# Attention scores from two float32r halves of q and k, projected with doubled weight columns

## The chip, the cores and the metric

The kernel runs on one core of one Trainium2 chip. The metric is the device time of one execution in microseconds (us). The engines are TensorE (PE, matrix products), VectorE (DVE), ScalarE (ACT, one function per element, with a bias and a scale), GpSimd (POOL) and SyncE (SP, which issues most transfers). Matrix products go to PSUM, eight banks of 512 float32 per partition; everything else lies in SBUF.

## The reference

Two layers follow each other: an attention over a weighted adjacency, and a graph network of three SAGE layers on a thinned adjacency. The change concerns the scores of the attention:

```python
x: (16, 1024, 128)   adj: (16, 1024, 1024)   H, HD = 8, 16
q = (x @ Wq.T + bq).reshape(bt, n, H, HD).transpose(0, 2, 1, 3)
k = (x @ Wk.T + bk).reshape(bt, n, H, HD).transpose(0, 2, 1, 3)
v = (x @ Wv.T + bv).reshape(bt, n, H, HD).transpose(0, 2, 1, 3)
scores = jnp.einsum('bhnd,bhmd->bhnm', q, k) / math.sqrt(HD)
scores = jnp.where((adj == 0)[:, None, :, :], -jnp.inf, scores)
attn = jax.nn.softmax(scores, axis=-1) * adj[:, None, :, :]
attn = attn / (attn.sum(axis=-1, keepdims=True) + 1e-08)
ctx = jnp.einsum('bhnm,bhmd->bhnd', attn, v)      # then ctx @ Wo.T + bo
...
adj_d = _dilate(adj, mask)     # neighbours removed row by row, in order
h1 = _bn(relu(_sage(h0, adj_d, ...)))             # and h2, h3 likewise
return concat(h1, h2, h3) @ Wl + bl
```

Here x of the attention is the layer-normalised and rectified input. The removal of neighbours (dilation) needs the adjacency alone, so the kernel computes it beside the attention.

## The kernel before

`swept` does all of it in one pass. The attention goes over 256 turns: batch b (16), half c of the queries (2), block m of 128 keys (8). Each turn has two half-turns, one for each group g of four heads (heads 2j + g, j = 0 to 3). A half-turn does, in this order:

- `scores`: 16 small bfloat16 matmuls (L554) lay -1e30 on the pairs without an edge, from `never` and `nomask`; then four float32 matmuls (L560), one for each row group of 32 rows, add k times q. The 32 rows of a row group hold two heads. `qT` holds q twice, for g = 0 and g = 1, each with the rows of the other head set to zero by the scale `own`. The result fills two tiles of two banks each, all that the pool `ps_s` has.
- other work that was queued: for g = 0 the four transposes of the adjacency block of two turns later (`turn_over`, L505) into the one bank of `ps_m`; for g = 1 one step of the list `beside`.
- `values`: for the half-turn before, the value columns of each head times w (L487) and the sums of e (L492).
- two exponentials on ACT (L598, e from the scores), two products on DVE (L603, w = e times the turned adjacency). e and w have four buffers each, so two half-turns.
- for g = 0, on ACT, the copy of the turned block out of its bank (L508) and the mask `nomask` from it (L512).

Work for the next batch stands in generators on the list `beside`. Each yields the kind of place at which it wants to go on, and `go_on_with` continues the first whose kind fits: `True` is the place behind the scores of the second half-turn, "evict" the place behind the products, `False` the end of a half-turn. `prepare` makes layer norm, the transpose hT, and for each half c the projections `key` (L322, evicted by L324 on ACT into kT), `value` (L333) and `query` (L312, evicted twice by L315 on ACT into qT). `conclude` turns and projects the finished half (L395 copies the two accumulators, L401, L414, L424, and L429 adds to the input on DVE). All of these go through the one bank of `ps_m`, except in the first batch.

The dilation is another generator. `beside_attention` continues it behind each half-turn as long as its planned cost lies behind the share of the half-turns that are done. Its largest rows on ACT are L915 and L909, on DVE L900, L922 and L925.

After the attention, `judge` counts what would make the one pass invalid (an adjacency value that is not as assumed, a removal that had not settled, a softmax sum out of range) and sets a flag. If the flag is set, the whole slower program `walked` runs behind. Then come the three SAGE layers.

Of the kernel before, what the change touches and what calls it, by code (L numbers as in the profile page):

```python
# [10 lines left out]
F32 = mybir.dt.float32  # L11
BF = mybir.dt.bfloat16
F16 = mybir.dt.float16
# [8 lines left out]
P = 128  # L22
# [12 lines left out]
def swept(ctx: ExitStack, tc: tile.TileContext, t: dict, out: bass.AP, flag: bass.AP):  # L35
# [131 lines left out]
    def first_part(p1):  # L167
# [32 lines left out]
        names = ("Wk", "Wv", "Wq", "Wo")  # L200
        raw = pool.tile([P, 4, D], F32, name="raw", tag="kT")
        for i, name in enumerate(names):
            nc.sync.dma_start(raw[:, i, :], t[f"L0_gnn_{name}"])
        attn_w = one.tile([P, 4, D], F32, name="attn_w")
        wts = {name: attn_w[:, i, :] for i, name in enumerate(names)}
        bk = one.tile([P, 1], F32, name="bk")
        nc.sync.dma_start(bk, t["L0_gnn_bk"].rearrange("(d o) -> d o", o=1))

        own = one.tile([P, 2], F32, name="own")
        nc.vector.tensor_reduce(  # L210
            own,
            ident.rearrange("p (j g d) -> p g j d", g=2, d=HD),
            AX.XY,
            ALU.add,
        )
        bq = one.tile([P, 3], F32, name="bq")
        nc.sync.dma_start(bq[:, 2:3], t["L0_gnn_bq"].rearrange("(d o) -> d o", o=1))
# [3 lines left out]
        def turn_weights():  # L221
            wps = ps_d.tile([P, 4, D], F32, name="wps", tag="d")
            for i in range(4):
                nc.tensor.transpose(wps[:, i, :], raw[:, i, :], ident)
            yield
            nc.vector.tensor_copy(attn_w, wps)
            nc.vector.tensor_tensor(bq[:, 0:2], own, bq[:, 2:3].to_broadcast([P, 2]), ALU.mult)
            yield
# [15 lines left out]
        both = shared.tile([P, 4096], F32, name="both", tag="aT2")  # L244
# [8 lines left out]
        ]  # L253
        never = one.tile([P, P], BF, name="never")
# [37 lines left out]
        def prepare(b):  # L292
# [15 lines left out]
            kT = pool.tile([P, N], F32, name=f"kT_{b}", tag="kT")  # L308

            def query(c, bank=(ps_m, "m")):  # L310
                pq = bank[0].tile([P, 512], F32, name=f"pq_{b}_{c}", tag=bank[1])
                nc.tensor.matmul(pq, wts["Wq"], hT[:, c * HN : (c + 1) * HN], start=True, stop=True)  # L312
                yield "evict"
                for g in range(2):
                    nc.scalar.activation(  # L315
                        qTs[c][:, g, :], pq, AF.Identity, bias=bq[:, g : g + 1], scale=own[:, g : g + 1]
                    )

            def key(c, bank=(ps_m, "m")):
                cc = slice(c * HN, (c + 1) * HN)  # L320
                pk = bank[0].tile([P, 512], F32, name=f"pk_{b}_{c}", tag=bank[1])
                nc.tensor.matmul(pk, wts["Wk"], hT[:, cc], start=True, stop=True)  # L322
                yield "evict"
                nc.scalar.activation(kT[:, cc], pk, AF.Identity, bias=bk)  # L324
# [17 lines left out]
            if b == 0:  # L342
# [13 lines left out]
                yield from key(0)  # L356
                qTs = [pool.tile([P, 2, HN], F32, name=f"qT_{b}_0", tag="qT")]
                yield from query(0, (ps_d, "d"))
                yield from second
                ready[b] = (xt, qTs, kT, v1)  # L360
# [3 lines left out]
                yield from turned(1)  # L364
            else:
# [4 lines left out]
                for what in (key, value):  # L370
                    yield True
                    yield from what(0)

                yield "half 1"
                qTs = [pool.tile([P, 2, HN], F32, name=f"qT_{b}_0", tag="qT")]
                yield True
                yield from query(0)

            ready[b] = (xt, qTs, kT, v1)
            for what in (key, value):  # L380
                yield True
                yield from what(1)
            yield "half 0"
            qTs.append(pool.tile([P, 2, HN], F32, name=f"qT_{b}_1", tag="qT"))
            yield True
            yield from query(1)

        def conclude(b, c, acc, xt):

            yield False  # L390
            cx = small.tile([P, HB, H, HD], F32, name=f"cx_{b}_{c}", tag="cx", bufs=1)
# [78 lines left out]
        def go_on_with(*kinds):  # L470


            for steps in beside[::-1] if kinds == ("first",) else beside:
                if steps[1] in kinds:
                    steps[1] = next(steps[0], None)
                    if steps[1] is None:
                        beside.remove(steps)
                    return

        def attention():  # L480
# [58 lines left out]
            def scores(i, g):  # L539
# [4 lines left out]
                _, qTs, kT, _ = ready[b]  # L544
                nomask = tiles[i][1]
                mm = slice(m * P, (m + 1) * P)
# [11 lines left out]
                for j in range(4):  # L558
                    rows = slice(32 * j, 32 * j + 32)
                    nc.tensor.matmul(  # L560
                        scs[j // 2][:, j % 2, :], kT[rows, mm], qTs[c][rows, g, :],
                        start=False, stop=True, tile_position=(32 * j, 0),
                    )
# [3 lines left out]
            for i, (b, c, m) in enumerate(turns):  # L567
# [12 lines left out]
                for g in range(2):  # L580
# [6 lines left out]
                    else:  # L587
                        go_on_with(True)
                    if late:
                        values(*late)  # L590
                    elif g == 0:
# [21 lines left out]
                    go_on_with(False)  # L613
                    if i + g + 1 < len(turns):
# [36 lines left out]
        def dilation():  # L651
# [84 lines left out]
            for k in range(NB):  # L736
# [150 lines left out]
                wrs, gms, ers, ets = {}, {}, {}, {}  # L887
# [8 lines left out]
                for i in range(B + 2):  # L896
# [15 lines left out]
                    if b < B:  # L912
                        wrs[b] = pool.tile([P, N], F16, name=f"wr_{k}_{b}", tag="wr", bufs=2)
# [1061 lines left out]
```

## Time and profile before

| What | us |
|---|---|
| median of 3 runs (lowest, highest) | 3412.89 (3412.76, 3414.29) |
| the profiled execution | 3414.15 |
| its span | 3412.3 |
| PE busy | 3316.5 (97%) |
| DVE busy | 2967.2 (87%) |
| ACT busy | 2328.2 (68%) |
| mean granted TensorE clock | 0.995 |

The profile is of one execution. Busy times are unions over the span; matmuls are pipelined and their ends are modelled, so the time that a group of matmuls takes is better read from start to start. The page shows 40 slices of 85.3 us with the busy tenths of each engine. A row of a group names line, engine, operation, output and inputs, shapes and count, then the busy time in us and the mean ns of one, then the idle time just before and what ended it. The attention takes the span up to about 2345 us; the SAGE layers take the rest.

### The profile page before, as it was taken

The numbers are of one execution on the slowest core, as the hardware profiler recorded it, in microseconds if no ns is written. First come the engines' busy times: TensorE is split into PE (matmuls) and PEld (weight loads), VectorE is DVE, ScalarE is ACT, GpSimd is POOL, SyncE is SP. The second block draws the span as 40 slices with busy tenths as digits, with TensorE's granted clock in tenths as the row PEclk, the third lists the DMA queues.
The fourth block names the chain that finished last, engine by engine and source line by source line (L and its number), as shares of the span: only waits on it lengthen the run. The fifth ranks groups of instructions, "written<-read, shape, count | busy, mean of one in ns | idle before, by whom it ended". The sixth has DMA issues, their size and how long they took to land. (4 is left out here: it accounts for less than half of the span.)

```text
span 3412.3 us, 86211 instructions
## 1 busy us (share of the span) xinstructions
PE 3316.5 (97%) x34855; PEld 1870.2 (55%) x34855; DVE 2967.2 (87%) x5271; ACT 2328.2 (68%) x3909; POOL 163.8 (5%) x253
## 2 busy tenths in 40 slices
PE   8999999999999999999999999999999899999997
PEld 3333333333333333333334334336999899999997
DVE  7888988988889898998988999897888799988887
ACT  7699689779879969968976986884222344433324
POOL 2000000000000000000000000000000000000000
PEclk9999999999999999999999999999999999999999
DMA  7366456547637745845863783677999799989996
GB/s 240 109 173 203 129 149 199 159 128 218 188 122 211 219 123 174 242 144 150 244 188 120 230 246 119 190 239 258 338 335 338 276 350 352 349 325 351 353 351 219
DMA packets 650122, 772.27 MB, mean 226 GB/s; under 512 B 173264, under 2 KB 569168, under 8 KB 637424
## 3 DMA queue, kind: packets, MB, share of 16 engines
q1 hardware_dynamic: 632672, 708.58, 64.2%
q0 software_dynamic: 15456, 57.30, 5.0%
q8 instruction: 275, 4.51, 0.6%
q14 instruction: 135, 1.11, 0.1%
q10 hardware_dynamic: 1584, 0.79, 0.1%
HBM read 508.50 MB, written 157.29 MB: 195 GB/s over the span
## 5 line engine op out<-in xcount | busy, mean ns | idle before, releaser
L603 DVE TENSOR_TENSOR w<-e,aT 128x1024 f32<-128x1024 f32 x1024 | 1206.1, 1219 | 193.3 <-ACT e L598 191.8
L598 ACT ACTIVATE e<-sc 128x1024 f32<-128x1024 f32 x1024 | 992.0, 1023 | 327.3 <-PE sc L560 326.2
L1129 PE MATMUL pg<-y,aT 128*128 128x128 f32 (+1 forms) x6144 | 729.8, 275 | 0.0
L1129 PEld LDWEIGHTS pg<-y,aT 128*128 128x128 f32 x6144 | 707.9, 192 | 0.0
L560 PE MATMUL sc<-qT,kT 32*128 32x512 f32 x4096 | 583.9, 640 | 0.5 <-ACT qT L315 0.5
L487 PE MATMUL acc<-w,both 128*32 128x512 f32 x4096 | 574.4, 605 | 5.8 <-DVE w L603 5.2
L492 PE MATMUL acc<-e,eps 128*32 128x512 f32 x4096 | 561.3, 593 | 0.0
L146 DVE SCALAR_TENSOR_TENSOR aT<-mr,aT 128x1024 f32<-128x1024 bf16 x384 | 458.9, 1217 | 0.0
L492 PEld LDWEIGHTS acc<-e,eps 128*32 128x32 f32 x4096 | 144.1, 110 | 299.7 <-issue 294.8
L1152 ACT ACTIVATE sq<-o 128x512 f32<-128x512 f32 x96 | 60.6, 631 | 356.1 <-DVE o L1147 356.1
L554 PE MATMUL sc<-nomask,never 32*32 32x512 bf16 x8192 | 268.0, 384 | 35.1 <-ACT e L598 32.0
L554 PEld LDWEIGHTS <-never 32*32 32x32 bf16 x8192 | 87.3, 87 | 376.5 <-issue 354.1
L1170 ACT COPY hT<-pt 128x512 f32<-128x512 f32 x96 | 56.4, 587 | 267.6 <-PE pt L1166 259.1
L560 PEld LDWEIGHTS sc<-qT,kT 32*128 32x128 f32 x4096 | 159.9, 182 | 116.9 <-issue 116.1
L505 PEld LDWEIGHTS pa<-ident,a 128*128 128x128 f32 x1024 | 107.7, 141 | 181.2 <-issue 126.7
L915 ACT ACTIVATE wr<-both,th 128x512 f16<-128x512 f16 x256 | 205.1, 879 | 1.7 <-DVE both L900 1.5
L505 PE MATMUL pa<-ident,a 128*128 128x128 f32 x1024 | 168.3, 287 | 6.5 <-DMA a<-in_adj 5.8
L487 PEld LDWEIGHTS acc<-w,both 128*32 128x32 f32 x4096 | 88.4, 108 | 150.4 <-issue 50.4
L512 ACT ACTIVATE nomask<-aT 128x512 bf16<-128x512 f32 x256 | 161.3, 630 | 8.3
L1147 DVE SCALAR_TENSOR_TENSOR o<-pg,rdeg,mine 128x128 f32<-128x128 f32 x384 | 108.2, 345 | 56.5 <-PE pg L1129 53.2
L508 ACT COPY aT<-pa 128x512 f32<-128x512 f32 x256 | 153.0, 598 | 5.0 <-PE pa L505 4.3
L900 DVE TENSOR_TENSOR_SCAN both<-rk 128x513 f16<-128x513 bf16 x128 | 155.9, 1218 | 0.0
(228 smaller groups left out, 3830.2 us busy)
## 6 DMA issues: line engine op xcount, KB each, us to landing
aT<-aT_d SPq DMA_DIRECT2D x94, 2048.0 KB, 9.9
mr<-mr_d SPq DMA_DIRECT2D x188, 512.0 KB, 6.2
aT_d<-aT SPq DMA_DIRECT2D x256, 256.0 KB, 4.3
a<-in_adj SPq DMA_DIRECT2D x253, 256.0 KB, 4.3
ad<-in_adj SPq DMA_DIRECT2D x112, 512.0 KB, 4.4
nomask<-nomask SPq DMA_DIRECT2D x512, 96.0 KB, 2.7
nomask<-nomask SPq DMA_DIRECT2D x512, 64.0 KB, 2.9
nomask<-nomask SPq DMA_DIRECT2D x512, 32.0 KB, 2.9
```

The costliest lines, as they stand in the source:

```text
L146: nc.vector.scalar_tensor_tensor(part, mrs[h][:, j : j + 2, :].rearrange("p j n -> p (j n)"), 0.0, part, ALU.is_equal, ALU.mult)
L487: nc.tensor.matmul(acc[g][32 * j : 32 * j + 32, :], v1[:, m, (2 * j + g) * HW : (2 * j + g) * HW + 32], ws[j // 2][:, j % 2, :], start=(m ...
L492: nc.tensor.matmul(acc[g][32 * j : 32 * j + 32, :], eps8, es[j // 2][:, j % 2, :], start=False, stop=(m == NB - 1),)
L505: nc.tensor.transpose(pa[:, k * P : (k + 1) * P], a[:, k, :], ident)
L512: nc.scalar.activation(nomask[:, 0, :], aT[:, 0, :], AF.Relu, bias=1.0, scale=-1e38, accum_out=zeros[:, i : i + 1])
L554: nc.tensor.matmul(scs[j // 2][to : to + 32, j % 2, :], never[rows, rows], nomask[rows, j, :], start=True, stop=False, tile_position=(32 * ...
L560: nc.tensor.matmul(scs[j // 2][:, j % 2, :], kT[rows, mm], qTs[c][rows, g, :], start=False, stop=True, tile_position=(32 * j, 0),)
L598: nc.scalar.activation(e, scs[q], AF.Exp, scale=1.0 / math.sqrt(HD))
L603: nc.vector.tensor_tensor(w, es[q], aT.to_broadcast([P, 2, HN]), ALU.mult)
L900: nc.vector.tensor_tensor_scan(pair_sums[b % 2], row[:, 0::2], row[:, 1::2], 0.0, ALU.add, ALU.add)
L915: nc.scalar.activation(wrs[b][:, t::2], pair_sums[b % 2][:, t : t + HN], AF.Abs, bias=at[:, b : b + 1], scale=2.0,)
L1129: nc.tensor.matmul(pg[:, i // 2, at : at + width], aT[:, j, i * P : (i + 1) * P], y[:, j, :width], start=(j == 0), stop=(j == NB - 1),)
```

## The change

q and k are kept as float32r, which the kernel takes for a float32 that is rounded when an engine writes it. Each number is held as a rounded high half and a residual, itself rounded. For this the projection weights of q and k are laid out anew by `twofold`: for each group g a matrix whose 32 columns of a row group hold one head's 16 columns twice. One projection per group then puts a head on both halves of the 32 rows. For k the upper 16 rows hold the rounded value and the lower 16 the residual (`key_halves`; `low_rows` is 1 on the lower rows). For q the high half stands on all 32 rows in one tile and the residual on all 32 in another (`query_halves`). The scores then are two matmuls per row group, k with q's high half and k with q's residual, eight in all instead of four, each with float32r operands.

So every projection of q and k is done twice, once for each group, and each is evicted by ACT (the rounded value) and then by DVE (value minus rounded value). In the schedule a projection's first matmul is issued at a new place, "end", at the end of a first half-turn; its eviction is at "early", in front of the exponentials of the second half-turn; its second matmul at "behind", after that half-turn's values; and the second eviction at "evict". `value` of the second half now goes ahead of `key` of the second half. To make room, the concluded context (`cx_home`) and the new weights lie in the tile `both`, and two tiles of the dilation share one (`pair`). `judge` also rounds a sample on ACT and on DVE and sets the flag where the two differ.

```diff
+        both = shared.tile([P, 4096], F32, name="both", tag="aT2")
+        one_w = one.tile([P, 2, D], F32, name="one_w")
+        two_w = both[:, 4096 - 4 * D :].rearrange("p (i d) -> p i d", d=D)
+        wts = {name: one_w[:, i, :] for i, name in enumerate(("Wv", "Wo"))}
+        wts |= {name: two_w[:, i, :] for i, name in enumerate(("q0", "q1", "k0", "k1"))}
+        bqk = one.tile([P, 4, 2], F32, name="bqk")
+        def twofold(dst, w):
+
+            for g in range(2):
+                of_g = w.rearrange("p (j g d) -> p g j d", g=2, d=HD)[:, g]
+                nc.vector.tensor_copy(
+                    dst[:, g, :].rearrange("p (j i d) -> p j i d", i=2, d=HD),
+                    of_g.unsqueeze(2).to_broadcast([P, 4, 2, HD]),
+                )
...
+            bps = ps_o.tile([P, HN], F32, name="bps", tag="acc0")
+            for g in range(2):
+                nc.tensor.matmul(
+                    bps[:, 2 * g : 2 * g + 2], twice_ident[:, g, :], bqk[:, 0, :], start=True, stop=True
+                )
-            nc.vector.tensor_copy(attn_w, wps)
-            nc.vector.tensor_tensor(bq[:, 0:2], own, bq[:, 2:3].to_broadcast([P, 2]), ALU.mult)
+            twofold(two_w[:, 2:4, :], wps[:, 3, :])
+            twofold(two_w[:, 0:2, :], wps[:, 2, :])
+            nc.vector.tensor_copy(one_w, wps[:, 0:2, :])
+            nc.vector.tensor_copy(bqk[:, 1:3, :].rearrange("p g t -> p (g t)"), bps[:, 0:4])
+            nc.vector.tensor_scalar(bqk[:, 3, :], bqk[:, 1:3, 1], low_rows, None, ALU.mult)
...
+        free += 2 * (HN // 2 + 1)
+        cx_home = both[:, free : free + HN]
+        twice_ident = shared.tile([P, 2, P], F32, name="twice_ident", tag="s", bufs=2)
+        twofold(twice_ident, ident)
...
-            kT = pool.tile([P, N], F32, name=f"kT_{b}", tag="kT")
-
-            def query(c, bank=(ps_m, "m")):
-                pq = bank[0].tile([P, 512], F32, name=f"pq_{b}_{c}", tag=bank[1])
-                nc.tensor.matmul(pq, wts["Wq"], hT[:, c * HN : (c + 1) * HN], start=True, stop=True)
-                yield "evict"
+            qs, ks = [], []
+
+
+
+            def query_halves(c, g, ps):
+                if g == 0:
+                    qs.append(pool.tile([P, 2, 2, HN], F32R, name=f"q_{b}_{c}", tag="qM"))
+                high, low = (qs[c][:, g, i, :] for i in range(2))
+                bias = bqk[:, 1 + g, 0:1]
+                nc.scalar.activation(high, ps, AF.Identity, bias=bias)
+                nc.vector.scalar_tensor_tensor(low, ps, bias, high.bitcast(F32), ALU.add, ALU.subtract)
+
+            def key_halves(c, g, ps):
+                if g == 0:
+                    ks.append(pool.tile([P, 2, HN], F32R, name=f"k_{b}_{c}", tag="kA", bufs=3))
+                half = ks[c][:, g, :]
+                nc.scalar.activation(half, ps, AF.Identity, bias=bqk[:, 3, g : g + 1], scale=low_rows)
+                nc.vector.scalar_tensor_tensor(
+                    half, ps, bqk[:, 1 + g, 1:2], half.bitcast(F32), ALU.add, ALU.subtract
+                )
+
+            def both_groups(name, halves, c, banks):
                 for g in range(2):
-                    nc.scalar.activation(
-                        qTs[c][:, g, :], pq, AF.Identity, bias=bq[:, g : g + 1], scale=own[:, g : g + 1]
+                    where, tag = banks[g % len(banks)]
+                    ps = where.tile([P, 512], F32, name=f"p{name}_{b}_{c}_{g}", tag=tag)
+                    nc.tensor.matmul(
+                        ps, wts[f"{name}{g}"], hT[:, c * HN : (c + 1) * HN], start=True, stop=True
                     )
-
-            def key(c, bank=(ps_m, "m")):
-                cc = slice(c * HN, (c + 1) * HN)
-                pk = bank[0].tile([P, 512], F32, name=f"pk_{b}_{c}", tag=bank[1])
-                nc.tensor.matmul(pk, wts["Wk"], hT[:, cc], start=True, stop=True)
-                yield "evict"
-                nc.scalar.activation(kT[:, cc], pk, AF.Identity, bias=bk)
+                    yield ("early", "evict")[g]
+                    halves(c, g, ps)
+                    if g == 0:
+                        yield "behind"
+
+            def query(c, banks=((ps_m, "m"),)):
+                yield from both_groups("q", query_halves, c, banks)
+
+            def key(c, banks=((ps_m, "m"),)):
+                yield from both_groups("k", key_halves, c, banks)
...
             else:
                 yield from layer_norm_relu(h, xt, f"a{b}")
                 for c in range(2):
                     yield True
                     yield from turned(c)
-                for what in (key, value):
-                    yield True
-                    yield from what(0)
-
+                yield "end"
+                yield from key(0)
+                yield True
+                yield from value(0)
                 yield "half 1"
-                qTs = [pool.tile([P, 2, HN], F32, name=f"qT_{b}_0", tag="qT")]
+                yield "end"
+                yield from query(0)
+                ready[b] = (xt, qs, ks, v1)
                 yield True
-                yield from query(0)
-
-            ready[b] = (xt, qTs, kT, v1)
-            for what in (key, value):
-                yield True
-                yield from what(1)
+                yield from value(1)
+                yield "end"
+                yield from key(1)
             yield "half 0"
-            qTs.append(pool.tile([P, 2, HN], F32, name=f"qT_{b}_1", tag="qT"))
-            yield True
+            yield "end"
             yield from query(1)
...
 
             yield False
-            cx = small.tile([P, HB, H, HD], F32, name=f"cx_{b}_{c}", tag="cx", bufs=1)
+            cx = cx_home.rearrange("p (i h d) -> p i h d", h=H, d=HD)
...
-                _, qTs, kT, _ = ready[b]
+                _, qs, ks, _ = ready[b]
                 nomask = tiles[i][1]
-                mm = slice(m * P, (m + 1) * P)
+                mm = slice(m % HB * P, (m % HB + 1) * P)
...
-                for j in range(4):
-                    rows = slice(32 * j, 32 * j + 32)
-                    nc.tensor.matmul(
-                        scs[j // 2][:, j % 2, :], kT[rows, mm], qTs[c][rows, g, :],
-                        start=False, stop=True, tile_position=(32 * j, 0),
-                    )
+                for half in range(2):
+                    for j in range(4):
+                        rows = slice(32 * j, 32 * j + 32)
+                        nc.tensor.matmul(
+                            scs[j // 2][:, j % 2, :], ks[m // HB][rows, g, mm], qs[c][rows, g, half, :],
+                            start=False, stop=(half == 1), tile_position=(32 * j, 0),
+                        )
...
                         turning = turn_over(i + 2)
                         next(turning, None)
                     else:
-                        go_on_with(True)
+                        twice_over = go_on_with("early")
+                        if not twice_over:
+                            go_on_with(True)
                     if late:
                         values(*late)
+                        if g == 1 and twice_over:
+                            go_on_with("behind")
                     elif g == 0:
                         go_on_with(True)
                     if (i, g) == (2, 0):
@@ -611,6 +658,8 @@
                     if g == 0:
                         next(turning, None)
                     go_on_with(False)
+                    if g == 0 and next((kind for _, kind in beside if kind in (True, "end")), None) == "end":
+                        go_on_with("end")
                     if i + g + 1 < len(turns):
                         made["next"] = partial(scores, i + g, 1 - g)
                     yield
...
-                        wrs[b] = pool.tile([P, N], F16, name=f"wr_{k}_{b}", tag="wr", bufs=2)
+                        pairs[b] = shared.tile([P, 2, N], BF, name=f"pair_{k}_{b}", tag="mr", bufs=4)
+                        wrs[b] = pairs[b][:, 0, :].bitcast(F16)
...
-                        er = ers[b] = pool.tile([P, N], BF, name=f"er_{k}_{b}", tag="er", bufs=3)
+                        er = ers[b] = pairs.pop(b)[:, 1, :]
...
+
+            rounded = small.tile([P, 2, D], F32R, name="rounded", tag="oT", bufs=2)
+            nc.scalar.copy(rounded[:, 0], sample)
+            nc.vector.tensor_copy(rounded[:, 1], sample)
+            words = rounded.bitcast(F32)
+            nc.vector.scalar_tensor_tensor(
+                words[:, 0], words[:, 0], 0.0, words[:, 1], ALU.add, ALU.not_equal, accum_out=still[:, 2:3]
+            )
+            nc.vector.tensor_tensor(still[:, 0:1], still[:, 0:1], still[:, 2:3], ALU.add)
```

## The prediction

> **What bounds the kernel now.** I read the page's busy shares and 40 slices first, then the groups of instructions of the attention part (0 to 2345 us), the waits, one stretch of the timeline, and the busy time in stretches of 50 us.
>
> ```profile
> PE   8999999999999999999999999999999899999997
> DVE  7888988988889898998988999897888799988887
> ACT  7699689779879969968976986884222344433324
> ```
>
> TensorE (PE) stands at 9 in nearly every slice, but in the attention part (slices 1 to 27) VectorE (DVE) is at 8 and 9 and ScalarE (ACT) swings between 6 and 9. All three are near full, so what one saves is worth only the distance to the next.
>
> ```profile
> L603 DVE TENSOR_TENSOR w<-e,aT 128x1024 f32<-128x1024 f32 x1024 | 1206.1, 1219 | 193.3 <-ACT e L598 191.8
> L598 ACT ACTIVATE e<-sc 128x1024 f32<-128x1024 f32 x1024 | 992.0, 1023 | 327.3 <-PE sc L560 326.2
> L560 PE MATMUL sc<-qT,kT 32*128 32x512 f32 x4096 | 583.9, 640 | 0.5 <-ACT qT L315 0.5
> L322 PE MATMUL pk<-hT,attn_w 128*128 128x512 f32 x64 | 36.9, 659 | 0.7 <-ACT aT L508 0.7
> L315 ACT ACTIVATE qT<-pq,bq,own 128x512 f32<-128x512 f32 x64 | 46.5, 788 | 0.9 <-PE pq L312 0.9
> L324 ACT ACTIVATE kT<-pk,bk 128x512 f32<-128x512 f32 x32 | 22.2, 693 | 1.7 <-PE pk L322 1.7
> L429 DVE TENSOR_TENSOR xt<-xt,pr 128x512 f32<-128x512 f32 x32 | 21.9, 685 | 16.1 <-PE pr L424 16.1
> ```
>
> A half-turn (one block, one group of heads) is one set of scores, two exponentials and two products, 512 of them. ACT waited 326 us for scores, DVE 192 us for exponentials; the scores waited for almost nothing. The 2048 score matmuls stand as 4096 records: a float32 matmul is two records.
>
> ```profile
> 1002.12 0.38 PE L112 MATMUL pv<-bias,ones_bf 3*128 3x512 bf16 x1
> 1002.42 1.16 PE L333 MATMUL pv<-attn_w,hT 128*128 128x128 f32 x8
> 1005.36 0.43 PE L554 MATMUL sc<-nomask,never 32*32 32x512 bf16 x16
> 1005.73 1.14 PE L560 MATMUL sc<-qT,kT 32*128 32x512 f32 x8
> 1006.80 0.66 PE L505 MATMUL pa<-ident,a 128*128 128x128 f32 x4
> 1007.38 1.06 PE L487 MATMUL acc<-w,both 128*32 128x512 f32 x8
> 1009.24 0.43 PE L554 MATMUL sc<-nomask,never 32*32 32x512 bf16 x16
> 1010.67 1.12 PE L312 MATMUL pq<-hT,attn_w 128*128 128x512 f32 x2
> ```
>
> From start to start on PE: mask 0.37, scores 1.07 (1005.73 to 1006.80), turn of a block 0.58, values with their sums 1.86 us. The projection at 1010.67 is followed by values at 1011.73: 1.06 us.
>
> ```profile
> 800.00:850.00 50.00, 46.77 (x505) 17.25 (x498) 44.45 (x73) 49.84 (x88) 2.80 (x3) 1.00 0.73 210
> 1250.00:1300.00 50.00, 50.00 (x598) 18.96 (x582) 41.07 (x57) 33.94 (x51) 2.17 (x3) 1.00 0.43 131
> 1900.00:1950.00 50.00, 49.85 (x523) 18.33 (x515) 49.01 (x80) 49.61 (x76) 2.19 (x3) 1.00 0.84 246
> ```
>
> The columns are PE, weight loads, DVE, ACT, POOL, then the granted clock. Here the average breaks up: at 800 ACT is the full engine and PE has 3.2 us to spare; at 1250 PE alone; at 1900 all three. Over the 45 stretches from 50 to 2300 the means are PE 49.1, DVE 44.5, ACT 42.2, yet in 13 of them ACT is at 49.4 or more. There a faster PE buys nothing.
>
> **Scores.** Four float32 matmuls on four row groups become eight float32r ones. No row of this trace shows float32r. Eight records go in two rounds of four concurrent ones, 1.07/2 = 0.535 us a round; a round of the values, which loads 32 columns of weights instead of 128, is 1.86/4 = 0.465. So 96 columns cost 0.07, 128 cost 0.09, and streaming 512 columns 0.44, which for float32 I read as two passes of 0.22. A single-pass round is then 0.22 + 0.09 = 0.31, and the bfloat16 row agrees (L112, 0.30). Two rounds: 0.63 us, a saving of 0.44 per half-turn, 225 us over 512. Bounds: the bfloat16 step twice, 0.60 (saving 0.47); float32 speed for each of eight records, 1.07 (saving nothing). I take 0.63, nearest to the one-pass row. That the residual is kept in a second operand speaks for a format that is multiplied in one pass.
>
> The rounds hit the same row groups twice, and the 0.07 us between the two kinds of round show that the weight loads of a round are not hidden. The Trainium skill (TensorE: Matmul & The Clock Gate, Part 3, "What overlaps and what doesn't") has the rule behind it: a weight load overlaps running matmuls only in another row group. It speaks against this order, in which the same key weights are loaded again for the low half of q; by its packing model without exposed loads, about 0.23 us a round, the estimate would be 0.46 and the saving 312 us. No run here shows float32r loads yet.
>
> **Projections.** Every q and k half-batch is projected twice: 64 more at 1.06 = 68 us of PE. PE net: -225 + 68 = -157 us.
>
> **Evictions.** DVE gets 128 new 128x512 subtractions out of PSUM, none removed; the nearest row is L429, 0.685: +88 us. ACT had 46.5 + 22.2 = 68.7 us and gets 128 x 0.693 = 88.7: +20 us. This lies beside PE, but DVE and ACT are the cover, so it counts where they lead.
>
> **The sum by stretches.** A stretch of 50 us holds 11.1 half-turns (4.5 us each) and 1.4 added projections: PE -4.9 + 1.5, DVE +1.9, ACT +0.4. I added these to each of the 45 stretches and took the fullest engine. At 800 it is ACT with 50.2, at 1250 PE with 46.6, at 1900 DVE with 50.9. All together: 19 stretches led by DVE give 31 us, 11 by PE 41, 15 by ACT 4: 76 us, half of what PE saves.
>
> **The new place of the projections.** Before, a projection stood behind the scores of the second half-turn. Now the first of each pair is issued at the end of the first half-turn, in front of the next mask and scores on PE's queue, and it needs the one bank that ACT's copy of the turned block (L508) empties. After the last score, PE is through with turn and values at 0.58 + 1.86 = 2.44; ACT ends two exponentials at about 2.04, the copy at 2.63, so PE starts near 2.75: 0.3 us lost. Projection to 3.8, mask and scores to 4.8, next exponential 4.9. ACT is through with its mask (0.82) at 3.45, evicts k from 3.9 to 4.6, and so idles 0.45 + 0.3 = 0.75. The second projection waits for DVE's subtraction, which ends some 0.7 after those scores while the values run 1.86: nothing. With 0.3 on PE and 0.75 on ACT per pair (64 pairs, 1.4 a stretch) the 76 us become 53. Bounds: nothing (queued dilation work fills the gaps) and 1.75 of ACT with 0.8 of PE (ACT comes late with other copies in front): 76 and 17.
>
> **The rest.** The sums took the fullest engine at 100%; before, it averages 49.6 of 50, so 45 x 0.4 = 18 us stay lost. In 13 stretches the two fullest are then within 1 us, for which I take another 0.4 each: 5 us. The start runs two more projections and subtractions before the first scores: about 4 us. The added check of rounding in judge is a few small operations under the first layer's matmuls: 1 us. The shared buffers (pair, cx_home) keep or raise their counts, and no DMA is added beyond the same small loads: nothing; if the rows of pair come free late, that is a stall of a turn, 9 us. The layers after 2345 us are untouched.
>
> 53 - 18 - 5 - 4 - 1 = 25 us off the profiled 3414.15 (span 3412.3): 3389. The median of the runs is 1.3 lower: 3388.
>
> **Rivals.**
> 1. The gain is larger. Four buffers of e and w let dilation work fill the gaps, so the pairs cost nothing and only half the loss stays: 76 - 9 - 5 = 62 us, 3351. For it: DVE averages 44.5, with room. Against: the scores use all four banks of their pool, so ACT cannot run ahead.
> 2. Slower through the pairs' place. The step from copy to projection to scores is an ACT gap at the fullest places. At the upper price 17 - 28 = -11: 3424. It decides from about 0.7 us of lost time per pair beyond the work, where the (76 - 28) us over 64 pairs are eaten. For it: ACT is full in 13 stretches; at a first block two more copies (L395) stand before L508.
> 3. float32r gains no speed per record. The same sum with no saving, and the pairs, is -62, with the 28 about +90: 3503. For it: no row here has it.
> 4. The rounding check differs between ACT and DVE, the flag is set, and the second program, walked, runs behind the first: far over 5000, as it does the whole work again without the overlap.
>
> **Chances.** Forecast 0.50 (its own range 3370 to 3405), rival 1 0.17, rival 2 0.22, rival 3 0.08, rival 4 0.03. A measurement of this kernel can tell about 0.2%, 7 us, from no change. Faster by more: all of rival 1 and four fifths of the forecast, 0.57; the same: 0.11; slower: 0.32. The range reaches from a little below rival 1 to above rival 2, 3345 to 3440, and leaves out rivals 3 and 4 and the tails.
>
> **What the profile after would show.** Right: 4096 score records in rounds near 0.31 us, scores to next instruction 0.63; DVE near 46 of 50 in attention; the attention part ending near 2320; PE waits for L508's copy before the first projection of a pair. Wrong: rounds still at 0.53 (rival 3); ACT waiting for scores on more than 326 us in total with the end not earlier (rival 2); DVE leading everywhere with the end below 2290 (rival 1).

## The result and the profile after

The changed kernel takes **3460.07 us**, the median of four runs (3457.88 to 3464.41). The kernel before, run beside it, took 3413.59 us. The ratio is 1.0134, with a 95% interval of 1.0119 to 1.0149: some 46 us slower, above the predicted range. The profiled execution after has a span of 3456.0 us.

The page after, busy shares and slices (the first rows give engine, busy us, share of the span and instructions; each digit is the busy share of one of 40 equal slices in tenths):

```profile
PE 3245.2 (94%) x34987; PEld 1905.7 (55%) x34987; DVE 3052.3 (88%) x5410; ACT 2357.7 (68%) x3942; POOL 165.0 (5%) x253
PE   8998998999999899899999999999999899999997
DVE  8888988988898898998999999997888799988887
ACT  7699789779879978977986996895323343432334
```

From slice 28 on all three rows are as full as they were before; in the attention part PE now falls to 8 here and there, where it stood at 9 nearly throughout. So PE gained room, and no other engine filled it. The groups of the attention part after (line, engine, operation; count; busy us and mean ns of one; idle us just before them, and what ended it):

```profile
L645 ACT ACTIVATE e<-sc 128x1024 f32<-128x1024 f32 x1024 | 991.2, 1022 | 230.1 <-PE sc L603 229.6
L603 PE MATMUL sc<-q,k 32*128 32x512 f32 x4096 | 379.8, 445 | 0.0
L353 PE MATMUL pk<-hT,both 128*128 128x512 f32 x128 | 74.7, 668 | 36.2 <-ACT aT L550 32.8 <-DVE k L345 3.0
L344 ACT ACTIVATE k<-pk,bqk,low_rows 128x512 fp32r<-128x512 f32 x64 | 50.0, 781 | 39.1 <-PE pk L353 39.1
L345 DVE SCALAR_TENSOR_TENSOR k<-pk,bqk,k 128x512 fp32r<-128x512 f32 x64 | 47.8, 747 | 37.1 <-ACT k L344 37.0
L338 DVE SCALAR_TENSOR_TENSOR q<-pq,bqk,q 128x512 fp32r<-128x512 f32 x64 | 47.7, 745 | 18.4 <-ACT q L337 18.4
```

The scores did become cheap: the group L603 is 380 us of PE where L560 was 584, and ACT's waits for scores fell from 326 to 230 us. What is new stands in the other rows. The projections (L353) wait for ACT's copy of the turned block (L550), ACT's evictions (L344) wait for the projections, and DVE's subtractions (L345, L338) for ACT's evictions. It is a chain through one bank of PSUM, and every link of it waits. At its end, the turn of a later block (`pa`) waits for the second subtraction, 39 us on PE in all. The waits that carry it (engine, tile and line, releaser, then us in total, times, longest; PEld is the weight load, which stands ahead of its matmul on PE's queue):

```profile
ACT e L645 <- PE sc L603: 229.6, 223, 3.6
PEld pk L353 <- ACT aT L550: 59.3, 30, 3.6
PEld pq L353 <- ACT aT L550: 45.4, 31, 2.6
PE pk L353 <- ACT aT L550: 31.9, 21, 2.7
PE pq L353 <- ACT aT L550: 17.0, 15, 1.7
PE pa L547 <- DVE k L345: 19.7, 30, 0.8
PE pa L547 <- DVE q L338: 19.6, 31, 0.8
```

One pair in the timeline after shows the order (start, duration, engine, what runs, and in brackets the idle time before it):

```profile
294.61 1.04 PE L534 MATMUL acc<-e,eps 128*32 128x512 f32 x8
294.87 1.95 ACT L645 ACTIVATE e<-sc 128x1024 f32<-128x1024 f32 x2
296.68 0.62 ACT L550 COPY aT<-pa 128x512 f32<-128x512 f32 x1
297.36 1.12 PE L353 MATMUL pq<-hT,both 128*128 128x512 f32 x2 [1.71 <-ACT aT L550]
298.32 0.61 PE L956 MATMUL pe<-ident_bf,pair 128*128 128x128 bf16 x8
298.86 0.43 PE L596 MATMUL sc<-nomask,never 32*32 32x512 bf16 x16
299.22 0.74 PE L603 MATMUL sc<-q,k 32*128 32x512 f32 x8
299.87 0.69 ACT L337 ACTIVATE q<-pq,bqk 128x512 fp32r<-128x512 f32 x1
299.89 1.07 PE L529 MATMUL acc<-w,both 128*32 128x512 f32 x8
```

PE is through with the sums of the last half-turn at 295.65. ACT had dilation work ahead of its exponentials, so these start only at 294.87; the copy, third in its line, ends at 297.30. PE stands for 1.71 us, projects, turns a piece of the dilation, and makes the next scores at 299.22. The next half-turn's first exponential starts at 300.46, 5.6 us after this one's; before, a half-turn took 4.5 on average.

I then measured the time from one half-turn's first exponential to the next for all 512 half-turns of both traces and averaged by the block's place in its batch (c is the half, m the block in it; each place occurs 16 times).

| half-turn | before, us | after, us | sum of 16, us |
|---|---|---|---|
| first of (0,0), (0,1), (1,4), (1,6), where the first projection is | 4.71, 4.19, 4.13, 4.07 | 6.38, 5.25, 5.18, 5.08 | +77 |
| second of the same blocks | 4.45, 5.10, 4.64, 5.15 | 5.00, 5.04, 5.01, 4.85 | +9 |
| the other 384 half-turns together | | -0.11 each | -44 |

The first exponential comes 3.9 us later (24.0 against 20.0). From the start of the first exponential to the end of the last it takes 2351.5 us, against 2309. The layers behind attention take the same time as before, within 3 us. So all of the loss is in 128 of the 512 half-turns, and the other 384 keep only 0.11 us each of what PE saves there.

The stretches after (PE, weight load, DVE, ACT and POOL busy, granted clock, DMA share, GB/s):

```profile
800.00:850.00 50.00, 46.12 (x520) 18.78 (x513) 45.61 (x80) 49.84 (x88) 2.78 (x3) 0.97 0.72 211
1250.00:1300.00 50.00, 49.49 (x709) 21.77 (x696) 48.85 (x114) 36.20 (x57) 2.87 (x3) 1.00 0.40 123
1900.00:1950.00 50.00, 45.17 (x502) 17.52 (x502) 43.95 (x56) 45.14 (x67) 0.00 (x0) 1.00 0.62 187
```

At 1900 no engine is above 45.2 of 50. There is no fullest engine any more; the time goes into waits between them. A sum by the fullest engine doesn't show such waits.

### The profile page after: what moved, and what is told of

The parts are those of the page before. It is cut to its first block, busy times and chain, and to the rows that moved or that the text cites. A ratio compares the mean times of both kernels' runs of the same rounds, so it can differ in the third digit from the quotient of the medians.

```text
span 3456.0 us, 86700 instructions
## 1 busy us (share of the span) xinstructions
PE 3245.2 (94%) x34987; PEld 1905.7 (55%) x34987; DVE 3052.3 (88%) x5410; ACT 2357.7 (68%) x3942; POOL 165.0 (5%) x253
## 5 line engine op out<-in xcount | busy, mean ns | idle before, releaser
L529 PE MATMUL acc<-w,both 128*32 128x512 f32 x4096 | 619.6, 610 | 4.5 <-DVE w L650 2.4
L534 PE MATMUL acc<-e,eps 128*32 128x512 f32 x4096 | 598.3, 594 | 0.0
L603 PE MATMUL sc<-q,k 32*128 32x512 f32 x4096 | 379.8, 445 | 0.0
L534 PEld LDWEIGHTS acc<-e,eps 128*32 128x32 f32 x4096 | 155.4, 111 | 299.5 <-issue 289.7
L603 PEld LDWEIGHTS sc<-q,k 32*128 32x128 f32 x4096 | 155.7, 183 | 117.1 <-issue 116.9
L965 ACT ACTIVATE pair<-both,th 128x512 f16<-128x512 f16 x256 | 204.8, 876 | 2.4 <-DVE both L949 2.3
L529 PEld LDWEIGHTS acc<-w,both 128*32 128x32 f32 x4096 | 97.3, 108 | 155.4 <-DVE w L650 77.3
L550 ACT COPY aT<-pa 128x512 f32<-128x512 f32 x256 | 152.5, 596 | 4.9 <-PE pa L547 4.5
```

The lines of the kernel that those rows point to most:

```text
L529: nc.tensor.matmul(acc[g][32 * j : 32 * j + 32, :], v1[:, m, (2 * j + g) * HW : (2 * j + g) * HW + 32], ws[j // 2][:, j % 2, :], start=(m ...
L534: nc.tensor.matmul(acc[g][32 * j : 32 * j + 32, :], eps8, es[j // 2][:, j % 2, :], start=False, stop=(m == NB - 1),)
L603: nc.tensor.matmul(scs[j // 2][:, j % 2, :], ks[m // HB][rows, g, mm], qs[c][rows, g, half, :], start=False, stop=(half == 1), tile_positi ...
L965: nc.scalar.activation(wrs[b][:, t::2], pair_sums[b % 2][:, t : t + HN], AF.Abs, bias=at[:, b : b + 1], scale=2.0,)
```

## The experiments

Two readings stood against each other. By P the new place and the doubled work of the projections cost the time, and the scores' saving is there to be had. By W the saving of PE turns into waits by itself, since DVE and ACT are nearly full, and the pairs are of little weight.

**The scores alone.** Before, with q and k kept as rounded float32r, and every score matmul made twice at half weight. The residuals, the doubled projections and their place are left out.

```diff
+        nc.vector.tensor_scalar(own, own, 0.5, None, ALU.mult)
...
-            kT = pool.tile([P, N], F32, name=f"kT_{b}", tag="kT")
+            kT = pool.tile([P, N], F32R, name=f"kT_{b}", tag="kT")
...
-                for j in range(4):
+                for half in range(2):
+                    for j in range(4):
...
-                        start=False, stop=True, tile_position=(32 * j, 0),
+                            start=False, stop=(half == 1), tile_position=(32 * j, 0),
```

> The kernel before, with q and k written as float32r and each score matmul done twice with half of q, so eight float32r matmuls as in the change; projections, evictions and their places are as before. Left out: the residual halves. Theory P (the place of the projections eats the gain): the saving of PE stands alone here, 0.44 us per half-turn, and by the stretch sum without additions 107 us come off: about 3306. Rival W (PE's saving is worth little, because ACT and DVE are full): the changed kernel's half-turns without projections got only 0.11 us shorter, 512 of them give 56 us: about 3357 or above.

Measured: 3358.75 us, ratio 0.9828 (0.9810 to 0.9846), 59 us faster. W's figure holds, P's doesn't. PE saves 0.40 us in each half-turn, 206 us in all, and 59 come out. The waits show where much of the rest went, before (first three) and here (last three):

```profile
ACT e L598 <- PE sc L560: 326.2, 257, 6.9
DVE w L603 <- ACT e L598: 187.3, 206, 2.2
PEld acc L487 <- DVE w L603: 36.1, 69, 2.5
ACT e L601 <- PE sc L563: 256.3, 217, 6.5
DVE w L606 <- ACT e L601: 154.0, 182, 2.5
PEld acc L489 <- DVE w L606: 112.5, 257, 3.3
```

ACT's and DVE's waits fell by 70 and 33 us, while the weight loads of PE's values now wait 112.5 us for DVE's product, against 36.1 before. PE's idle time between the first and the last exponential grew from 45 to 101 us. Some of the rest went to the clock: 23.9 us of the attention part ran at half clock, against 3.4 before, which is worth up to 10 us.

**The place alone.** Before, in float32 and with one projection, which is issued at the end of the first half-turn and evicted in the second, as the change does. The scores stay as they were; there are no residuals and no second projection.

```diff
-                yield "evict"
+                yield "early"
...
-                yield True
+                yield "end"
                 yield from query(0)
...
-                        go_on_with(True)
+                        if not go_on_with("early"):
+                            go_on_with(True)
...
+                    if g == 0 and next((kind for _, kind in beside if kind in (True, "end")), None) == "end":
+                        go_on_with("end")
```

> The kernel before in float32, with one projection per half-batch as before, but issued at the end of the first half-turn and evicted in front of the exponentials of the second. Nothing else of the change. Theory P: each of the 64 costs 0.5 to 1.0 us, as PE waits for the copy of the turned block and ACT for projection and scores behind it: 3445 to 3475. Rival W: within 10 us of before, 3404 to 3424.

Measured: 3452.89 us, ratio 1.0098 (1.0081 to 1.0115), 35 us slower, as P has it. With nothing else changed, the first half-turns of the four blocks go from 4.71, 4.19, 4.13 and 4.07 us to 6.45, 5.79, 5.33 and 5.65, 98 us in all. The second ones, from which the projection is gone, get 59 us shorter. The wait is the same one:

```profile
PEld pk L322 <- ACT aT L515: 50.6, 30, 2.8
PEld pq L312 <- ACT aT L515: 38.2, 31, 1.9
```

One thing differs from the change: both evictions of q stand in front of the exponentials here, where the changed kernel has one of them. In the next experiment, also in float32, one of the two stands later: the half-turns with q (the second and fourth of the four) take 5.42 and 5.32 us there, 0.35 less, and those with k 6.44 and 5.33, the same as here. Over 32 half-turns this can be up to 11 of the 35 us.

**The second projection.** The kernel of the place alone, with every float32 projection made twice and evicted twice to the same values: the pair's work, without float32r, without subtractions.

```diff
-                yield "early"
                 for g in range(2):
+                    yield ("early", "evict")[g]
...
+                    if g == 0:
+                        yield "behind"
+                        pq = bank[0].tile([P, 512], F32, name=f"pq2_{b}_{c}", tag=bank[1])
+                        nc.tensor.matmul(pq, wts["Wq"], hT[:, c * HN : (c + 1) * HN], start=True, stop=True)
```

> The kernel before in float32 with every projection made twice at the changed places (first at the end of the first half-turn, second behind the values of the second), no float32r, no subtractions on DVE; q's two groups are evicted from one projection each, k's is evicted twice into the same place. Beside the run with the place alone (3453) it adds the second projection. Theory S (the second projection costs its time on PE, since PE is the full engine): 3453 + 64 x 0.7 to 1.06 = 3495 to 3520. With the scores' 59 us off and the subtractions' 14 to 17 on, that returns near the changed kernel's 3460. Rival H (the second projection hides where ACT or DVE lead): 3453 to 3470.

Measured: 3514.37 us, ratio 1.0291 (1.0274 to 1.0308), 100 us over before and 65 over the place alone, each against the kernel before as run beside it. In this float32 kernel PE is the fullest engine, and the 64 x 1.06 = 68 us of projections are paid almost in full. What they cost where the scores leave PE more room, no run shows by itself.

**The subtractions.** The changed kernel without its 128 subtractions on DVE; both score rounds use the rounded q, and the low half is left out.

```diff
-                nc.vector.scalar_tensor_tensor(low, ps, bias, high.bitcast(F32), ALU.add, ALU.subtract)
...
-                nc.vector.scalar_tensor_tensor(
-                    half, ps, bqk[:, 1 + g, 1:2], half.bitcast(F32), ALU.add, ALU.subtract
-                )
...
-                            scs[j // 2][:, j % 2, :], ks[m // HB][rows, g, mm], qs[c][rows, g, half, :],
+                            scs[j // 2][:, j % 2, :], ks[m // HB][rows, g, mm], qs[c][rows, g, 0, :],
```

> The changed kernel without the 128 subtractions on DVE; places, both projections and ACT's evictions as changed, score matmuls eight as changed (both with the rounded q). Left out: the residuals. Theory P: the place stays, so only part of the 46 us comes back: 3425 to 3450. Rival W: DVE's 88 us are the cause, and without them it is faster than before by 20 us or more: 3390 or below.

Measured: 3443.35 us, ratio to before 1.0069 (1.0052 to 1.0085). That is 26 us over before instead of 46: the 95.5 us of subtractions are worth about 21 us of the loss, and the kernel is slower without them too.

The four pieces stand to the whole so: 3414 - 59 (scores) + 35 (place) + 65 (second projection) + 21 (subtractions) = 3476, where 3460 was measured. They explain 16 us too much. Place and second projection were measured in float32, where PE has the least room, so each may be worth less in the changed kernel.

**The old place again.** The changed kernel with one projection for both groups (the second group's weights are left out), issued where it was before, with its four evictions in a row behind the products.

```diff
-                    yield ("early", "evict")[g]
                     halves(c, g, ps)
-                    if g == 0:
-                        yield "behind"
...
+                yield "evict"
...
-                yield "end"
+                yield True
                 yield from key(1)
```

> The changed kernel with one projection for both groups at the old place behind the scores of the second half-turn, and all four evictions (two on ACT, two on DVE) behind the products. Left out: the second group's projection; both groups take the first group's. Theory P: the place is gone and PE saves its 225 us, the stretch sum gives 64 us off: about 3350. Rival W: the 88 us of DVE and 20 of ACT are what costs, so little is won: 3400 or above.

Measured: 3497.77 us, ratio 1.0231 (1.0214 to 1.0248), 80 us slower. P's 3350 failed outright, and W's bound holds without its reason, so this run doesn't tell the two apart. It made a new stall:

```profile
PE pa L545 <- DVE k L345: 73.1, 30, 3.8
PE pa L545 <- DVE q L338: 64.2, 31, 3.5
```

The four evictions alternate between ACT and DVE and hold the one bank all the while, and the turn of the next block waits 137 us for it. With the waiting the clock fell, too: 164 us of the attention part ran at half clock, against 31 in the changed kernel, which is worth up to 67 us. How much of the loss is the stall itself and how much the clock is not separated, so the run does not show what the old place costs at full clock.

**The bank emptied earlier.** The changed kernel, with ACT's copy of the turned block between the two exponentials where a pair comes next, instead of behind both.

```diff
                 nc.scalar.copy(aT[:, 0, :], pa)
+                yield
...
                         es.append(e)
+                        if (g, q) == (0, 0) and next((kind for _, kind in beside if kind in (True, "end")), None) == "end":
+                            next(turning, None)
```

> The changed kernel, with the copy of the turned block out of its bank put between the two exponentials instead of behind them, in the half-turns that end with a first projection; nothing left out. Theory P1 (what costs at the new place is the wait for the copy): PE gets the bank one exponential, 1.0 us, earlier, where it waited; 30 to 45 us less, 3415 to 3430. Rival P2 (what costs is that projection stands in front of the scores at all): within 10 us of the changed kernel, 3450 to 3465.

Measured: 3427.73 us, ratio to before 1.0043 (1.0026 to 1.0059): 13 us over before instead of 46, so 33 us less. The first half-turns of the pairs go from 6.38, 5.25, 5.18 and 5.08 us to 5.06, 4.90, 4.79 and 4.69, and the wait for the copy halves:

```profile
PEld pk L353 <- ACT aT L550: 27.5, 26, 1.7
PEld pq L353 <- ACT aT L550: 24.9, 23, 1.7
```

PE's matmuls themselves wait 9.7 us for the copy (48.9 in the changed kernel). The wait for the bank is shown to be a cause, and with what follows from it, it is most of the 46 us. Part of what follows is the clock: 6.8 us of the attention part ran at half clock here, 30.7 in the changed kernel, so up to 12 of the 33 us. The turn still waits 42.1 us for the second subtractions.

**The same, with the place alone.** The float32 kernel with the moved projection, and the copy between the exponentials.

```diff
                 nc.scalar.copy(aT[:, 0, :], pa)
+                yield
...
+                        if (g, q) == (0, 0) and next((kind for _, kind in beside if kind in (True, "end")), None) == "end":
+                            next(turning, None)
```

> The kernel before in float32 with the place alone, as in the run that measured 35 us for it, and with the copy of the turned block between the two exponentials in the half-turns that end with a projection; nothing left out. Theory P1 (the wait for the copy is what the place costs): nearly all of the 35 us go, 3414 to 3428. Rival P2 (a projection in front of the scores costs its 1.06 us on ACT's chain, whatever the copy does): 3435 to 3455.

Measured: 3426.95 us (six runs), ratio to before 1.0039 (1.0023 to 1.0055). That is 12 us over before, so of the 35 us of the place some 23 are the late copy. The runs spread from 3418 to 3437, so the remainder is uncertain. The half-turns with q, which have two evictions in front of the exponentials, are the longer ones (5.49 and 5.32 us, with k 5.18 and 5.08), which is part of it.

**The block turned first.** The changed kernel, with the next block turned and copied in front of a half-turn's own scores where a pair comes, so that the bank is free long before the projection.

```diff
+                    if g == 0:
...
+                        pair = not pair and i > 0 and pair_next()
+                        turning = turn_over(i + 2)
+                        if pair:
+                            next(turning, None)
+                            next(turning, None)
                     scs = scores(i, g)
...
+                        if pair:
+                            go_on_with("end")
```

> The changed kernel, nothing left out, with the pair of projections taken out of the way of the scores: in three of the four pairs of a batch the adjacency block is turned and copied in front of the half-turn's own scores, so the bank is free early; the first projection then stands behind those scores and in front of the values, its evictions behind that half-turn's exponentials and products, the second projection as changed. The fourth pair, which follows another directly, has the copy between the exponentials as in the run before. Theory P (place): what the first half-turns of these three pairs still cost in the run with the copy between, 26 us, goes away, and the turn in front of the scores costs at most 48 x 0.58 = 28 in PE-led places but less elsewhere: 3400 to 3420, about level with the kernel before. Rival: two projections, subtractions and evictions fill PE, DVE and ACT wherever they stand: 3422 to 3435.

Measured: 3447.86 us, ratio 1.0100 (1.0083 to 1.0117). Both expectations were too low.

```profile
PE pa L547 <- DVE k L345: 35.5, 30, 2.7
PEld pa L547 <- ACT both L378: 25.3, 27, 1.1
```

Now it is the turn that waits, for the evictions of the half-turn ahead of it, and since it stands in front of the scores, the scores wait with it. Every order tried pays for the one bank somewhere.

**The scores once.** Before, with rounded q and k and four float32r matmuls; the residuals and the second round are left out.

```diff
-            kT = pool.tile([P, N], F32, name=f"kT_{b}", tag="kT")
+            kT = pool.tile([P, N], F32R, name=f"kT_{b}", tag="kT")
...
-                qTs = [pool.tile([P, 2, HN], F32, name=f"qT_{b}_0", tag="qT")]
+                qTs = [pool.tile([P, 2, HN], F32R, name=f"qT_{b}_0", tag="qT")]
```

> The kernel before with q and k written as float32r and one float32r matmul per row group, four instead of eight; places and projections as before. Left out: the residuals altogether, so the scores come from rounded q and k. Theory F (PE's saving is worth only what ACT and DVE leave): the first 0.44 us per half-turn gave 59 us, another 0.3 gives little: 3335 to 3355. Rival L (each us of PE is worth the same): 59 x 0.75 / 0.44 = 100 off, 3315.

Measured: 3343.48 us, ratio 0.9786 (0.9769 to 0.9802), 71 us faster. It is the fastest of all, but its scores come from rounded q and k, as they do in the first experiment; neither computes what the change is for. A score group takes 0.437 us here against 0.669 for two rounds, and the 0.23 us that go, 119 us over 512 half-turns, bring 15 us (3358.75 to 3343.48; 12 by the ratios). But 78.5 us of the attention part ran at half clock here, against 23.9 in the first experiment, which is worth up to 27 us. So it isn't shown that PE's time at the scores is worth so little at full clock.

## Why the prediction was wrong, point by point

- **Scores, mechanism right, size a little off.** From scores to the next instruction the median is 0.669 us (predicted 0.63), against 1.072 before: 0.40 us per half-turn, 206 us, where the prediction had 0.44 and 225. The Trainium skill (TensorE: Matmul & The Clock Gate, Part 3) led to an estimate of 0.46 for the two rounds; the measurement decides against it. From the first round's start to the second's it is 0.338 us, which agrees with the rule that loads into busy row groups aren't hidden. Leaving out a round saves only 0.23, though, so what such a load costs isn't settled.
- **The sum by stretches failed, and was the largest miss.** This is the step that counts PE's saving, over 50 us, down to the next fullest engine. Done without any addition it gives 130 us for the scores, 107 after the 18 and 5 us set aside as never regained; measured were 59, so it was 48 us too high. The 0.04 us by which the saving of a half-turn was overestimated make 5 of them. A stretch of 50 us holds eleven half-turns and lets an engine that is early in one make up in another, but the buffers couple the engines at every half-turn. Done half-turn by half-turn on the trace of before, with 0.40 us saved, the same sum gives 68. That the grain is the reason is argued from this agreement; no run changes the buffers. Up to 10 us more went to the clock, for which the prediction has no term.
- **The additions were too low.** Projections, evictions and subtractions were to cost 130 - 76 = 54 us, the pairs' place 23, the start and the check 5: 82 us in all. Measured are the 46 us of the whole and the 59 of the scores, 105: 23 us more. Within this the subtractions were near: without them the prediction's sum comes to 102 us instead of 76, so they cost 26 there, and about 21 were measured. The second projection was not: without it the sum comes to 87, so it costs 11 there, and 65 were measured, though in float32. The single prices were near as well: a subtraction took 0.747 us instead of 0.685, ACT's evictions 94 us in all where 89 were predicted. The "nothing" for the second projection's wait behind DVE's subtraction was nearly right (7.6 us on PE), but the prediction has no term for the turn that waits for the second subtraction, 39 us on PE.
- **The pairs' place, mechanism right, mis-sized.** The prediction took 0.3 us of PE for the wait for L508's copy, worked out for an ACT that comes to the copy at once, and let it cost 23 us (76 to 53). After, PE's matmuls waited 48.9 us in 64 pairs, 0.76 each. By the trace nearly all of it falls in 36 pairs, in which ACT came to its exponentials more than 0.3 us after the scores or had other work between them and this copy; in 26 others, where it came promptly, PE lost 1.5 us in all. So the late ACT, which the prediction had as a bound, was the more frequent case. By itself, in float32, the place costs 35 us, with the second eviction of q in it.
- **Rival 2 came nearest.** It had the sign, and the place as a cause, priced at 3424. It did not say that the scores' saving itself would be worth so little, which is the larger part of the miss. The sign that it named in the profile did not appear: ACT's waits for scores fell to 230 us instead of going over 326. The loss stands in PE's waits for the copy instead. The forecast's other signs are seen in part: PE does wait for the copy, and DVE is near 46 at 800 (45.61), but the last exponential ends at 2375.5 instead of near 2320.
- **Rivals 1, 3 and 4** are out: the pairs do cost time, float32r is faster per round, and there is no second program in the span.
- **The rest.** The later start was 3.9 us (4 predicted), and the layers behind attention are untouched, as predicted. The drop of the clock was not foreseen; it is worth up to 15 us in the changed kernel (below).

In sum, the 25 us predicted off became 46 on, a miss of 71: the scores brought 48 us less than the sum made of them, and all that the change adds beside them cost 23 more. Of the two readings W holds for the scores and P for the place.

What stays open: how the 105 us divide between place, second projection and subtractions in the changed kernel itself, since the single pieces add up to 121; and what remains of the place with the earlier copy. A second bank for the projections was not tried.

## What to carry to other kernels

Sum a saving at the grain at which buffers couple the engines, here the half-turn, and not over a stretch that holds many: here 68 came out by half-turns, 107 by stretches, and 59 was measured. The room seen in a longer stretch need not be at hand where added work falls. Count the uses of a bank that everything goes through: before, 32 half-turns of a batch held 32 uses of this one (16 turned blocks, 16 others), and the change needs four more, so that in four places two uses share a half-turn. Where that can't be avoided, empty the bank as early as its engine can (33 us here), and put nothing that waits for it in front of the step that feeds the next engine. Where PE comes to wait more, look at the granted clock before explaining a time: in two of the runs here (the old place, the scores once) it fell enough to change what the run can show.

## What the runs showed of the hardware

- Four concurrent float32r matmuls (32 rows, 128 columns of weights, 512 streamed) start 0.338 us before the next four. In float32 the same four matmuls stand as eight records, whose two lots of four start 0.533 us apart, and the next instruction starts 1.072 us after the first. A lone float32r round of four has its successor 0.437 us after its start.
- The clock fell to half for stretches of 3.413 us or a few times that. Between the first and the last exponential the trace of before has 3.4 us at half clock, the place alone 3.4, the early copy 6.8, the scores alone 23.9, the changed kernel 30.7 (9 stretches), the scores once 78.5, and the old place with four evictions 164. A stretch of 3.413 us costs at most 1.7 us, so this is up to 15 us in the changed kernel. Half-turns at half clock were in fact longer than others at the same place in their batch, by 0.4 to 0.65 us for each us at half clock (0.41 in the changed kernel, 0.51 with the scores alone, 0.52 at the old place, 0.64 with the scores once; a fit over the 512 half-turns of each trace).
- In the changed kernel the 3.4 us ahead of such a stretch held 0.5 to 2.6 us of idle PE, and for 4 of the 9 no single gap was over 0.9 us. The Trainium skill (TensorE: Matmul & The Clock Gate, Part 1) gives the same window length; for mid-kernel drops it names idle gaps above some 3.4 us and, for one other kernel, frequent short idling. Several short gaps came before these drops here. No run isolates the trigger, and it stays open.
